# Moving operand sums between GpSimd and VectorE, and splitting layernorm steps over other ticks, in an attention + LoRA block

## The chip, the cores and the metric

One core of a Trainium2 chip runs the whole program. The metric is device microseconds of that core, the median of several runs. The engines are named as the profile names them: PE (TensorE), DVE (VectorE), ACT (ScalarE), POOL (GpSimd) and SP (SyncE, which issues the DMAs here).

## The reference

The input is 8 batches of 512 rows of 1024 numbers, all float32.

```
x = x + layernorm(attn(layernorm(x)) @ Wo)       # 16 heads of 64, rotary q and k, causal softmax
h = layernorm(x)
x = x + layernorm(h @ W.T + bias + use_lora * (h @ A[b].T) @ B[b].T)   # three adapters of rank 16
```

## The kernel before, in words

**Two phases.** The first runs 32 attention units (8 batches, 4 groups of 4 heads). A unit is 21 ticks long; at each tick a piece of the q, k, v products of the next unit is issued between the pieces of attention. The last unit has no next one, so PE runs attention alone there. The second phase (`with ExitStack() as a` on) multiplies by a 1024x1024 matrix 16 times: passes q = 0 to 7 are batch q times Wo, passes 8 to 15 are batch q-8 times the FFN weight. Each pass ends in layernorm and residual, row tile by row tile, during the pass after it; for q < 8 the rows are normed once more and transposed to be the operand of pass q+8.

**Products.** Each multiplication is done by a scheme of seven products in place of eight (Strassen, in Winograd's form), twice nested. The left operand is the weight (`LW`, tiles `wo_..`, `wf_..`), the right one the rows (`RX`, tiles R and T). Of its four quarters the weight has L11, L12, L21, L22 and the sums S1 = L21+L22, S2 = S1-L11, S3 = L11-L21 (in place of L21), S4 = L12-S2. The rows have R11, R12, R21, R22 and T1 = R12-R11, T2 = R22-T1, T3 = R22-R12 (in place of R12), T4 = R21-T2. Each of these tiles has seven slots: four sub-quarters and three sums of them, which `sub_left` (L665) and `sub_right` (L698) form inside a tile. `sum_left` (L677) forms one of four parts of an S tile, `sum_right` (L710) one of three pieces of a T tile (slots 0-1, 2-3, 4-6).

**Ticks and slots.** A pass has 49 ticks: seven groups of seven slots. The groups are, in ORDER, (L11,R11), (L12,R21), (L22,T4), (S1,T1), (S3,T3), (S2,T2), (S4,R22), so they begin at ticks 0, 7, 14, 21, 28, 35, 42. A slot is one sub-product of two matmuls of 256 columns. In SLOTS the sub-products use the accumulators b, a, c (this one still for the group before), c, d, b, a. Accumulator a has one buffer, as d has; b and c have two.

**Drains.** `Group.drain` empties them a tick after the sub-product: at slot 2 ACT copies a to `p1` (L847) and DVE forms `u2` = p1 + b (L843); at slot 3 DVE finishes the group before; at slot 6 DVE does three adds (p1 + b, + c, + d); at slot 0 of the next group ACT copies a (L854). So the next group's slot 1 waits for that copy, slot 5 (which goes on adding to b) for `u2`, slot 2 of the next group (which goes on adding to c) for the first of the adds to c, slot 4 of the next for that to d.

**What sets the order.** Every engine has its own queue in program order, written by `run(tick, filler)` (L528): at a tick come the PE events, then the sub-product and the drain of the one before, then the other events in the order in which they were entered. Nothing is scheduled by a tool. A tick number thus decides the order in a queue; the time comes from semaphores alone. An engine with an empty queue runs ahead of PE as far as its operands allow.

**What the change touches.** Before the last unit's run the first weight (Wo) and right operand (pass 0) are loaded on SP in the order L11, R11, L12, R21, R12, R22, L22, L21. POOL does all `sub_left` and the sums S1 and S3 there, and DVE does T1, T2, T4, T3 at the unit's ticks 18 to 21. S2 and S4 follow on POOL in pass 0. Four sums over the last heads' results (L499, POOL) and a store to memory end the unit. `plan_right` plans the right operand of the next pass: loads at ticks 10, 17, 24, 31, T1, T2, T4 at 38, 45, 52 and T3 at 63 (tick 14 of the pass itself). `plan_left` loads the second weight in pass 7 and plans its sums in passes 7 and 8. `load_ht` and `sub_ht` (L799, L800) bring the small LoRA operand `htb` with its differences on POOL; slot 4 of a pass's second group is the first to use it. `combine` (L860) adds whole 128x1024 result tiles, in pass q at ticks 18, 38 and 45 to 52; POOL does c21, DVE the rest. `plan_rows` plans the norms of a pass: for row tile t from tick k = 55 + 7t on (tick 6 + 7t of the next pass). `stats` forms bn statistics of two halves (L875), their aggregate (L878) on DVE, a square root on ACT (L880), reciprocal and scaled mean (L885, L887) on DVE; `norm` (L892, ACT) applies them to a half; `add_row` (L904, POOL) adds the residual; `store_rows` (L909, SP) stores it. For q < 8 a second norm follows (key `x`), then PE transposes (L918), ACT copies to `xT` (L922), the LoRA input product (L928) and the store of `xT` to `x1t` (L942). `plan_last` is the same for the last pass, by itself.

Of the kernel before, what the change touches and what calls it, by code (L numbers as in the profile page):

```python
# [13 lines left out]
ALU = mybir.AluOpType  # L14
# [4 lines left out]
B, S, E = 8, 512, 1024  # L19
# [6 lines left out]
HALF = 512  # L26
# [102 lines left out]
def sandwich_kernel(  # L129
# [589 lines left out]
    for u in range(U):  # L719
# [10 lines left out]
        else:  # L730
# [14 lines left out]
            for n in ("L11", "L12", "L22", "S3"):  # L745
                for k in range(4):
                    sub_left("wo", n, k, eng)
            for n in ("S1", "S3"):
                for h in range(4):
                    sum_left(wop, "wo", n, n, h, eng)  # L750
            for k, n in enumerate(("T1", "T2", "T4", "T3")):
                events[base + 18 + k].append(lambda n=n: sum_right(gp, 0, n, nc.vector))
# [8 lines left out]
    with ExitStack() as a:  # L761
# [109 lines left out]
        def stats(key, srcs, step):  # L871
# [4 lines left out]
            if step == 1:  # L876
                mv = small.tile([P, 2], F32, tag="mv", name=f"mv_{key}")
                nc.vector.bn_aggr(mv, ln[key])  # L878
                sd = small.tile([P, 1], F32, tag="sd", name=f"sd_{key}")
                nc.scalar.activation(sd, mv[:, 1:2], AF.Sqrt, bias=eps, scale=1.0)  # L880
                ln[key] = mv, sd
            if step == 2:
# [18 lines left out]
        def add_row(q, t, eng=None):  # L901
            for h, c in enumerate(halves(q, t)):
                e = eng or nc.gpsimd
                e.tensor_tensor(c, c, row[q, t][:, ts(h, HALF)], op=ALU.add)  # L904
# [57 lines left out]
        def plan_left(base):  # L962
# [13 lines left out]
            for n, tag, eng, ticks in (  # L976
                ("S1", "S3", pool, (43, 44, 45, 46)), ("S3", None, dve, (58, 61, 65, 68)),
                ("S2", "S2", pool, (57, 59, 61, 63)), ("S4", "S4", pool, (70, 72, 74, 76)),
# [9 lines left out]
        def plan_rows(q, base):  # L988

            for t in range(NT):  # L990
                k = base + 55 + 7 * t
                key = f"{'o' if q < B else 'y'}{q}_{t}"
                at(k, lambda t=t: load_row(q, t))
                for m in range(3):
                    at(k + m, lambda t=t, m=m, key=key: stats(key, halves(q, t), m))
                at(k + 3, lambda t=t, key=key: [norm(key, c, c) for c in halves(q, t)])
                at(k + 4, lambda t=t: add_row(q, t))
                at(k + 11, lambda t=t: store_rows(q, t))
                if q < B:
                    key = f"x{q}_{t}"  # L1000
                    for m in range(3):
                        at(k + 13 + m, lambda t=t, m=m, key=key: stats(key, halves(q, t), m))
                    at(k + 16, lambda t=t, key=key: [
                        norm(key, row[q, t][:, ts(h, HALF)], c) for h, c in enumerate(halves(q, t))
                    ])
# [189 lines left out]
```

## Time and profile before

| | |
|---|---|
| median of 3 runs | 2663.11 us (2663.02 to 2663.95) |
| the profiled execution's own time | 2664.64 us |
| its span, from the first to the last instruction | 2662.6 us |
| mean granted TensorE clock | 0.986 |
| second phase, first PE row | 1765.74 us |
| pass 7 and 8, POOL busy from 2154.90 to 2277.40 us | 120.83 of 122.50 us |
| PE busy in the same stretch | 92.39 us |

The page gives busy times of each engine, then the span in 40 slices of 66.6 us, each digit a busy share in tenths. A line of a timeline is: start, duration, engine, line, operation, output <- input, shape, count, and in brackets the idle time just before and the instruction that ended it. "+2 forms" or a count over one means that rows are merged, so a duration is that of all of them from the first's start. A line of the waits is: engine, tile and line that waited <- what it waited for: total us, times, longest.

### The profile page before, as it was taken

How to read it: one execution, taken by the hardware profiler on the slowest of the kernel's cores; microseconds unless marked ns; L12 is line 12 of the kernel's file. 1: busy time of each engine (PE TensorE's matmuls, PEld its weight loads, DVE VectorE, ACT ScalarE, POOL GpSimd, SP SyncE). 2: the span in 40 equal slices, each digit the busy share in tenths (PEclk: the TensorE clock that was granted, in tenths of full speed). 3: DMA queues.
4: the chain of work that ended last, by engine and by line, in shares of the span. 5: the costliest groups of instructions: out<-in, count | busy, mean ns of one | idle time of the engine just before them, and what ended most of it. 6: DMA issues, size and time to landing. Idle time of an engine off the chain costs nothing.

```text
span 2662.6 us, 40719 instructions
## 1 busy us (share of the span) xinstructions
PE 2544.0 (96%) x14656; PEld 2072.2 (78%) x14656; DVE 1577.5 (59%) x3702; ACT 1060.5 (40%) x2674; POOL 1534.2 (58%) x1141
## 2 busy tenths in 40 slices
PE   7999999999999999999999999969999986999997
PEld 6778777787778777878788778738777775888886
DVE  5655555554565455555565555446667665676666
ACT  1544444444454354444344434323434432322222
POOL 5364444436436436445443554386776699788885
PEclk9999999999999999999999999979999998999999
DMA  4232423423423333242342232235456562423433
GB/s 151 96 108 85 147 64 108 146 73 106 138 75 113 113 107 99 84 143 66 111 143 87 91 111 84 91 146 166 166 193 207 199 215 91 156 99 135 152 110 131
DMA packets 95130, 326.75 MB, mean 123 GB/s; under 512 B 16753, under 2 KB 18801, under 8 KB 77522
## 3 DMA queue, kind: packets, MB, share of 16 engines
q1 hardware_dynamic: 94930, 324.15, 36.7%
q8 instruction: 118, 1.93, 0.3%
q14 instruction: 82, 0.67, 0.1%
HBM read 208.74 MB, written 81.79 MB: 109 GB/s over the span
## 4 chain that ended last, share of the span: by engine, by line
PE 85%; DVE 7%; POOL 4%; issue 2%; ACT 1%; DMA 1%; SPq 0%; ACTq 0%; DVEq 0%; POOLq 0%
PE s L399 7%; PE ptp L455 6%; PE po L475 6%; PE accc_P L821 6%; PE acca_P L821 5%; PE accb_P L821 5%; PE acca_q L348 5%; PE acca_v L330 4%; PE accb_k L348 4%; PE accc_q L348 4%; PE accc_k L348 4%; PE acca_k L348 4%; PE accb_q L348 4%; PE accc_v L330 4%; PE accb_v L330 4%; PE accd_P L821 3%
## 5 line engine op out<-in xcount | busy, mean ns | idle before, releaser
L430 ACT ACTIVATE pr<-pr,nm 128x128 f32<-128x128 f32 (+3 forms) x512 | 282.2, 552 | 576.0 <-DVE nm L420 576.0
L441 ACT ACTIVATE pr<-pr,rs 128x128 f32<-128x128 f32 (+3 forms) x512 | 252.2, 552 | 161.1 <-DVE rs L438 161.1
L420 DVE CUSTOM_DVE_ANT_0 pr<-s,mask 128x128 f32<-128x128 f32 (+3 forms) x512 | 225.8, 488 | 92.1 <-PE s L399 91.4
L181 POOL TENSOR_TENSOR sv<-wv 128x512 f32<-128x512 f32 x32 | 40.6, 1269 | 316.1 <-PE accc_q L348 316.1
L904 POOL TENSOR_TENSOR c<-c,row 128x512 f32<-128x512 f32 x120 | 164.8, 1394 | 88.0 <-ACT c L892 85.0
L455 PE MATMUL ptp<-ident,pr 128*128 128x128 f32 x1280 | 186.2, 281 | 17.7 <-ACT pr L441 17.7
L399 PE MATMUL s<-k,q 64*128 64x128 f32 (+3 forms) x1024 | 193.0, 474 | 1.6 <-DVE nm L420 1.3
L710 POOL TENSOR_TENSOR T<-R,T 128x512 f32<-128x512 f32 (+1 forms) x90 | 165.5, 1866 | 38.8 <-PE accc_P L821 24.8
L455 PEld LDWEIGHTS ptp<-ident,pr 128*128 128x128 f32 x1280 | 147.6, 142 | 50.9 <-ACT pr L441 34.0
L181 POOL TENSOR_TENSOR sq<-wq 128x512 f32<-128x512 f32 x32 | 40.6, 1267 | 241.1 <-PE accc_k L348 234.9
L181 POOL TENSOR_TENSOR sk<-wk 128x512 f32<-128x512 f32 x32 | 41.3, 1290 | 198.5 <-PE accc_v L330 198.5
L475 PE MATMUL po<-pT,v 128*64 128x512 f32 (+3 forms) x1024 | 154.7, 443 | 0.0
L330 PEld LDWEIGHTS acca_v<-wv,R 128*128 128x128 f32 x1024 | 119.3, 192 | 23.6 <-issue 23.5
L467 DVE COPY pT<-ptp 128x384 f32<-128x384 f32 (+1 forms) x128 | 79.5, 621 | 95.0 <-PE ptp L455 92.4
L475 PEld LDWEIGHTS po<-pT,v 128*64 128x64 f32 x1024 | 69.0, 138 | 85.7 <-issue 71.6
L348 PE MATMUL acca_q<-R,wq 128*128 128x256 f32 x512 | 128.1, 393 | 0.0
L330 PE MATMUL acca_v<-wv,R 128*128 128x128 f32 x1024 | 127.9, 278 | 0.0
L348 PEld LDWEIGHTS acca_q<-R,wq 128*128 128x128 f32 x512 | 92.7, 191 | 44.0 <-issue 33.8
L843 DVE TENSOR_TENSOR p_P<-accb_P,p_P 128x256 f32<-128x256 f32 x112 | 46.9, 419 | 125.5 <-PE accb_P L821 71.2
L348 PE MATMUL acca_k<-R,wk 128*128 128x256 f32 x512 | 121.0, 379 | 0.0
L348 PEld LDWEIGHTS acca_k<-R,wk 128*128 128x128 f32 x512 | 96.7, 190 | 12.9
L399 PEld LDWEIGHTS s<-k,q 64*128 64x128 f32 x1024 | 73.2, 187 | 42.7 <-issue 34.7
(266 smaller groups left out, 6541.3 us busy)
## 6 DMA issues: line engine op xcount, KB each, us to landing
wq<-in_wq_dram SPq DMA_DIRECT2D x32, 1024.0 KB, 5.1
wk<-in_wk_dram SPq DMA_DIRECT2D x32, 1024.0 KB, 4.9
wv<-in_wv_dram SPq DMA_DIRECT2D x32, 1024.0 KB, 5.0
attn<-ops SPq DMA_DIRECT2D x16, 1792.0 KB, 7.9
R<-attn SPq DMA_DIRECT2D x32, 896.0 KB, 4.8
x<-in_x_dram SPq DMA_DIRECT2D x32, 512.0 KB, 7.4
row<-in_x_dram SPq DMA_DIRECT2D x32, 512.0 KB, 6.0
x<-c SPq DMA_DIRECT2D x64, 256.0 KB, 3.6
```

Source lines behind the costliest of these rows:

```text
L181: lambda eng: eng.tensor_tensor(s1, L21, L22, op=ALU.add),
L330: nc.tensor.matmul(acc[:, ts(c, P)], lhsT=R[right][:, k, ts(c, P)], rhs=L[left][:, k, :], start=(first and c == 0 and k == 0), stop=True, ...
L348: nc.tensor.matmul(acc, lhsT=L[left][:, k, :], rhs=R[right][:, k, :], start=(first and k == 0), stop=True, skip_group_check=True,)
L399: nc.tensor.matmul(ps[:, j, at : at + L], lhsT=qT[r, self.i, ts(qb, P)], rhs=kT[r, self.i, :L], start=True, stop=True,)
L420: nc.vector.tensor_tensor_reduce(out=v[:, j, :], in0=self.ps[qb][:, j, :], in1=mask[:, S - L :], scale=-1.0 / HD**0.5, scalar=3.0e38, op0= ...
L430: nc.scalar.activation(v[:, j, :], v[:, j, :], AF.Exp, bias=nm[:, j : j + 1], scale=-1.0, accum_out=sm[:, j : j + 1],)
L441: nc.scalar.mul(v, v, rs[:, j : j + 1])
L455: nc.tensor.transpose(pt[:, n, :], self.pr[qb][:, j, ts(kb, P)], ident)
L475: nc.tensor.matmul(po[j * HD : (j + 1) * HD, kb * P :], lhsT=v[:, kb, c : c + HD], rhs=self.pT[j][:, kb, kb * P :], start=(kb == 0), stop= ...
L710: eng.tensor_tensor(RX[q, n][:, c], RX[q, x][:, c], RX[q, y][:, c], op=ALU.subtract)
L821: nc.tensor.matmul(acc, lhsT=right[:, SLOT_R[r], k, :], rhs=left[:, SLOT_L[l], k, :], start=(first and k == 0), stop=True, skip_group_chec ...
L904: e.tensor_tensor(c, c, row[q, t][:, ts(h, HALF)], op=ALU.add)
```

## The change

The diff does four things.

- In the last attention POOL's queue gets T1, T2 and T4 of pass 0 between the differences of L12 and L22. S1 and S3 of the first weight leave it for DVE at ticks 15-18 and 20-23 of pass 0; S2 and S4 stay on POOL, at ticks 24 and 33 in place of 14 and 26; T3 goes to DVE at ticks 24 to 26 in three pieces.
- In `stats` the square root gets a step of its own, one tick after the aggregate. The steps of `plan_rows` move to suit: the halves' norms and adds stand at ticks of their own, the second norm's statistics begin at k+12 in place of k+13, rows are loaded at k+2 and stored at k+12.
- The second weight's S1 goes from POOL (ticks 43-46 of pass 7) to DVE (47, 50, 53, 54); the ticks of S3 and S2 move by one to two. Each sum is in four parts as before.
- For pass 8 alone, the LoRA operand is loaded at tick 10 of pass 7 and its differences formed at 16, in place of 52 and 53.

```diff
--- before.py
+++ after.py
@@ -742,14 +742,12 @@
             load_right(gp, 0, "R22")
             load_left(wop, wo, "wo", "L22", "L22")
             load_left(wop, wo, "wo", "L21", "S3")
-            for n in ("L11", "L12", "L22", "S3"):
-                for k in range(4):
-                    sub_left("wo", n, k, eng)
-            for n in ("S1", "S3"):
-                for h in range(4):
-                    sum_left(wop, "wo", n, n, h, eng)
-            for k, n in enumerate(("T1", "T2", "T4", "T3")):
-                events[base + 18 + k].append(lambda n=n: sum_right(gp, 0, n, nc.vector))
+            for n in ("L11", "L12", "T1", "T2", "T4", "L22", "S3"):
+                if n[0] == "T":
+                    sum_right(gp, 0, n, eng)
+                else:
+                    for k in range(4):
+                        sub_left("wo", n, k, eng)
             for k in range(PER + 1):
                 run(base + k, None)
             for k in sorted(events):
@@ -876,10 +874,13 @@
             if step == 1:
                 mv = small.tile([P, 2], F32, tag="mv", name=f"mv_{key}")
                 nc.vector.bn_aggr(mv, ln[key])
+                ln[key] = mv
+            if step == 2:
+                mv = ln[key]
                 sd = small.tile([P, 1], F32, tag="sd", name=f"sd_{key}")
                 nc.scalar.activation(sd, mv[:, 1:2], AF.Sqrt, bias=eps, scale=1.0)
                 ln[key] = mv, sd
-            if step == 2:
+            if step == 3:
                 mv, sd = ln[key]
                 rs = small.tile([P, 1], F32, tag="rstd", name=f"rstd_{key}")
                 nc.vector.reciprocal(rs, sd)
@@ -898,10 +899,9 @@
             src = x[q, ts(t, P), :] if q < B else x1d[q - B][:, t, :]
             nc.sync.dma_start(out=row[q, t], in_=src)
 
-        def add_row(q, t, eng=None):
-            for h, c in enumerate(halves(q, t)):
-                e = eng or nc.gpsimd
-                e.tensor_tensor(c, c, row[q, t][:, ts(h, HALF)], op=ALU.add)
+        def add_row(q, t, h):
+            c = halves(q, t)[h]
+            nc.gpsimd.tensor_tensor(c, c, row[q, t][:, ts(h, HALF)], op=ALU.add)
 
         def store_rows(q, t):
             for h, c in enumerate(halves(q, t)):
@@ -974,8 +974,8 @@
                         lambda n=n, m=m: sub_left("wf", "S3" if n == "L21" else n, m, pool),
                     )
             for n, tag, eng, ticks in (
-                ("S1", "S3", pool, (43, 44, 45, 46)), ("S3", None, dve, (58, 61, 65, 68)),
-                ("S2", "S2", pool, (57, 59, 61, 63)), ("S4", "S4", pool, (70, 72, 74, 76)),
+                ("S1", "S3", dve, (47, 50, 53, 54)), ("S3", None, dve, (59, 60, 66, 67)),
+                ("S2", "S2", pool, (58, 60, 62, 64)), ("S4", "S4", pool, (70, 72, 74, 76)),
             ):
                 for m in range(4):
                     at(
@@ -990,19 +990,21 @@
             for t in range(NT):
                 k = base + 55 + 7 * t
                 key = f"{'o' if q < B else 'y'}{q}_{t}"
-                at(k, lambda t=t: load_row(q, t))
-                for m in range(3):
+                at(k + 2, lambda t=t: load_row(q, t))
+                for m in range(4):
                     at(k + m, lambda t=t, m=m, key=key: stats(key, halves(q, t), m))
-                at(k + 3, lambda t=t, key=key: [norm(key, c, c) for c in halves(q, t)])
-                at(k + 4, lambda t=t: add_row(q, t))
-                at(k + 11, lambda t=t: store_rows(q, t))
+                for h in range(2):
+                    at(k + 4 + h, lambda t=t, h=h, key=key: norm(key, halves(q, t)[h], halves(q, t)[h]))
+                    at(k + 6 + h, lambda t=t, h=h: add_row(q, t, h))
+                at(k + 12, lambda t=t: store_rows(q, t))
                 if q < B:
                     key = f"x{q}_{t}"
-                    for m in range(3):
-                        at(k + 13 + m, lambda t=t, m=m, key=key: stats(key, halves(q, t), m))
-                    at(k + 16, lambda t=t, key=key: [
-                        norm(key, row[q, t][:, ts(h, HALF)], c) for h, c in enumerate(halves(q, t))
-                    ])
+                    for m in range(4):
+                        at(k + 12 + m, lambda t=t, m=m, key=key: stats(key, halves(q, t), m))
+                    for h in range(2):
+                        at(k + 16 + h, lambda t=t, h=h, key=key: norm(
+                            key, row[q, t][:, ts(h, HALF)], halves(q, t)[h]
+                        ))
                     for g in range(2):
                         at(k + 20 + g, lambda t=t, g=g: transpose_x1(q, t, g), "pe")
                         at(k + 20 + g, lambda pt, t=t, g=g: keep_x1(q, t, g, pt), "post")
@@ -1044,23 +1046,29 @@
                 at(base + 34, lambda t=t: load_row(q, t))
             for t in range(2):
                 at(base + 46 + t, lambda t=t: [ready(t, 0), ready(t, 1), moments_of(t)])
-                at(base + 47 + t, lambda t=t: [stats(f"y{q}_{t}", None, 2), end(t, 0, pool), end(t, 1, pool)])
+                at(base + 47 + t, lambda t=t: [stats(f"y{q}_{t}", None, 3), end(t, 0, pool), end(t, 1, pool)])
             at(base + 48, lambda: [load_row(q, 3), ready(2, 1)])
             at(base + 49, lambda: [sum_c12(0), ready(2, 0), moments_of(2), ready(3, 1)])
-            at(base + 52, lambda: [sum_c12(1), ready(3, 0), moments_of(3), stats(f"y{q}_2", None, 2),
-                                   stats(f"y{q}_3", None, 2)])
+            at(base + 52, lambda: [sum_c12(1), ready(3, 0), moments_of(3), stats(f"y{q}_2", None, 3),
+                                   stats(f"y{q}_3", None, 3)])
             at(base + 53, lambda: [end(2, 0, pool), end(2, 1, dve), end(3, 0, pool), end(3, 1, dve)])
 
-        for n, k in (("S2", 14), ("S4", 26)):
+        for n, k, eng in (
+            ("S1", 15, nc.vector), ("S3", 20, nc.vector), ("S2", 24, nc.gpsimd), ("S4", 33, nc.gpsimd)
+        ):
+            pool = wop if eng is nc.vector else wop2
             for h in range(4):
-                at(k + h, lambda n=n, h=h: sum_left(wop2, "wo", n, n, h, nc.gpsimd))
+                at(k + h, lambda n=n, h=h, eng=eng, pool=pool: sum_left(pool, "wo", n, n, h, eng))
+        for h in range(3):
+            at(24 + h, lambda h=h: sum_right(gp, 0, "T3", nc.vector, slice(h, h + 1)))
         for q in range(NQ):
             base = q * N2
             if q + 1 < NQ:
                 plan_right(q + 1, base)
             if q >= B - 1 and q + 1 < NQ:
-                at(base + 52, lambda q=q: load_ht(q + 1 - B))
-                at(base + 53, lambda q=q: sub_ht(q + 1 - B))
+                k = 10 if q == B - 1 else 52
+                at(base + k, lambda q=q: load_ht(q + 1 - B))
+                at(base + k + (6 if q == B - 1 else 1), lambda q=q: sub_ht(q + 1 - B))
             if q == B - 1:
                 plan_left(base)
             dve, pool = nc.vector, nc.gpsimd
```

## The prediction

> **What bounds the kernel now.** I read the page, then TensorE's waits from 1766 us on (the projection passes), then the timelines of all engines around each wait.
>
> ```profile
> PE 2544.0 (96%) x14656; PEld 2072.2 (78%) x14656; DVE 1577.5 (59%) x3702; ACT 1060.5 (40%) x2674; POOL 1534.2 (58%) x1141
> PE   7999999999999999999999999969999986999997
> ...
> POOL 5364444436436436445443554386776699788885
> ```
>
> TensorE (PE) is the bound; it falls off in slices 27 and 33-34, and in the latter POOL is full. Nothing can be won but PE's gaps. Those of the projection, as totals, counts and longest:
>
> ```profile
> PE acca_P L821 <- ACT c L854: 21.7, 16, 5.9
> PE accd_P L828 <- POOL htb L800: 21.5, 6, 15.3
> PE accb_P L821 <- DVE u_P L843: 13.9, 2, 13.7
> PE acca_P L821 <- ACT U L854: 11.3, 8, 6.0
> ```
>
> Gap A, at the start of pass 0 (start, duration, engine):
>
> ```profile
> 1754.13 8.19 POOL L677 TENSOR_TENSOR wo_S<-wo_L,wo_L 128x1024 f32<-128x1024 f32 x4
> 1766.46 5.72 DVE L710 TENSOR_TENSOR T<-R,R 128x512 f32<-128x512 f32 x3
> 1772.11 8.48 DVE L710 TENSOR_TENSOR T<-R,T 128x512 f32<-128x512 f32 x6
> 1780.51 2.15 DVE L710 TENSOR_TENSOR R<-R,R 128x512 f32<-128x512 f32 x3
> 1783.14 2.04 PE L821 MATMUL accb_P<-wo_L,R 128*128 128x256 f32 x4 [13.68 <-DVE u_P L843]
> 1785.09 8.19 POOL L677 TENSOR_TENSOR wo_S<-wo_S,wo_L 128x1024 f32<-128x1024 f32 x4 [5.17 <-DMA attn<-ops]
> ```
>
> Twelve right-operand sums stand on DVE ahead of the first drain, and PE idles 13.68 us. Gap B, once in each of passes 1 to 7 with two small ones:
>
> ```profile
> 1946.32 2.00 DVE L860 TENSOR_TENSOR c<-c,A 128x1024 f32<-128x1024 f32 x1
> 1950.68 0.21 DVE L878 BATCH_NORM_AGGREGATE mv_x<-bn_x 128x2 f32<-128x12 f32 x1
> 1950.92 0.29 ACT L880 ACTIVATE sd_x<-mv_x,eps 128x1 f32<-128x1 f32 x1 [3.74 <-DVE mv_x L878]
> 1951.12 0.35 ACT L854 COPY c<-acca_P 128x256 f32<-128x256 f32 x1
> 1951.53 1.13 PE L821 MATMUL acca_P<-wo_S,T 128*128 128x256 f32 x4 [1.59 <-ACT c L854]
> ```
>
> ACT holds a square root that waits for DVE; the copy that frees accumulator `a` stands behind it. Gaps C, passes 7 and 8:
>
> ```profile
> 2195.88 2.08 PE L821 MATMUL acca_P<-wo_S,R 128*128 128x256 f32 x4 [5.99 <-ACT U L854]
> 2224.67 6.21 POOL L710 TENSOR_TENSOR T<-R,T 128x512 f32<-128x512 f32 x3
> 2232.68 1.22 PE L828 MATMUL accd_P<-lb_sb,htb 128*128 128x256 f32 x2 [15.34 <-POOL htb L800]
> 2251.93 2.07 PE L821 MATMUL acca_P<-wf_S,T 128*128 128x256 f32 x4 [5.94 <-ACT c L854]
> ```
>
> From 2154.9 to 2277.4 POOL is busy 120.8 of 122.5 us: the stretch is POOL's.
>
> **What the Trainium skill says.** "SBUF — State Buffer", Who interferes with whom: a DVE instruction with two SBUF inputs and a GpSimd one that reads SBUF exclude each other, one blocking fully. The trace agrees: the 128x1024 combine takes 1.22 us at best and 2.0-2.2 beside POOL; T1's three pieces took 5.72 us beside POOL, T3's, alone, 2.15. Drains (one input in PSUM) stay at 0.41-0.43. "TensorE: Matmul & The Clock Gate", What's actually happening: an idle window of some 3.4 us halves PE's clock. Agrees: after the gaps of 6 us and more PE's first rows take 2.08 and 1.91 where 1.03 is usual, about 2.6 us lost each. Same page, Architectural detail: DVE and ACT are strict FIFOs; gap B shows it.
>
> A tick (two sub-products) is 0.863 us by PE's starts.
>
> **Startup (A).** Removed: the 9 pieces of T1, T2, T4 on DVE (5.72 + 8.48 us) and T3 there (2.15). POOL takes the nine in the last attention at 1.25, 1.25, 1.8 us a sum (a later T1 on POOL: 4.27), 12.9 in all, and is rid of S1 and S3 there (8.19 + 9.08, from 1754.13 to 1771.37). Its last weight differences would end near 1764 and the last heads' four sums, which wait for DVE's store at 1766.5, near 1772 instead of 1778.6: hidden by attention, unless the right operand's loads land after 1744, when L22, queued behind them on SP, had landed; each us later than about 2 us would then be one on the heads' sums, which pass 0 doesn't need. The first drain is at 1768.7; the 13.68 us and 2.6 of slow clock go. Added on DVE in ticks 15-26: S1, S3 (three parts of 1.15 and one of 0.6 each, 4.05), T3 (2.1), beside the combine of tick 18 (1.15). Behind them stand the drains, for which PE waits. POOL's S2 and S4 (2.3, 2.3, 2.3, 1.27 a sum) follow S1 part by part whatever their tick, since POOL is empty; they take turns with DVE. The walk, DVE's piece first wherever it is queued already: S1 starts 1777.6; S1 part 3 ends 1785.8; combine 1789.9 (behind a POOL part); S3 parts 1792.3, 1795.7, 1799.2, so the `u2` drain for tick 26 is at 1799.6, 6.4 us late; last piece of T3 between 1802 and 1805.5. Tick 28 needs that piece. Before it began at 1805.66, so 0 to 4 us are won, less 1-2 of slow clock after the new gap. I take **1 us**; the ends are +12 (POOL comes late and DVE runs alone: T3 ends at 1793) and -4 (each turn is a full POOL part and the clock falls twice).
>
> **Square roots (B).** Aggregate and square root keep a tick between them, and x statistics start a tick earlier, ahead of the combine. In the second and fourth tile the aggregate now precedes the three drains of its tick (1.2 us): gaps of 0.63 and 0.57 vanish. In the first, the statistic goes to tick 18, but the combine still waits for POOL's T3, itself 0.8 us later as the reciprocal moved: aggregate 0.7 us earlier, 1.59 becomes 0.9. Each half's norm costs 0.77 as before (1.52 a pair), between copies. Pass 1 gains 1.5 (its gap is 1.01), passes 2-6 1.9 each: **11 us**. Ends: 6 (the first tile gains nothing and one small gap stays) and 13 (all close). Adds, row loads and row stores move 1-4 ticks, hidden: tile t's add ends some 3 us before its statistics, as POOL idles 4-5 us per tile there.
>
> **The weight change (C).** Off POOL: S1 (5.65 + 3.56 = 9.2). The LoRA differences (0.72 + 0.99) move ahead, to tick 16; their load, on SP at tick 10, reads rows written in pass 1 and waits for nothing, so the row and weight loads behind it on SP lose only its issue (0.45 us, hidden by their slack). On DVE: S1, 4.05, each part excluding POOL. S1's second part needs L22's third difference from POOL, with `u2` of tick 51 queued behind it.
> - 5.99: the fourth tile's add now stands behind two weight differences more (2.5), the LoRA pair (1.7) and 0.8, so at 2193.7, not 2188.7; its statistics are asked for a tick earlier and hold DVE. PE's tick 43 stays at about 2196: gain 0. (The other cause, rows stored ahead of `x1t` on SP, goes, as they change places.)
> - 15.34: the LoRA operand is ready. Late next is T4 on POOL, before done at 2230.84: less 9.2, plus 2.5 (LoRA, reciprocal), plus 4.05 of blocking: 2228.2; walking the turns gives up to 2230.4. Tick 63 goes from 2237.19 to 2229.5: gain 7.7.
> - 5.94: add, S2 and S3 take turns as before; tick 71 from 2251.93 to between 2244 and 2248: gain 4-8 (T3's and S3's pieces stand in DVE's way as before; POOL reaches the first tile's add up to 8 us earlier).
> - 0.63 and 1.91 close, the third tile's add costs some 4: by tick 92 (2282.00 before) 8 to 12. I take **10 us**, pass 7's own B gaps included. Ends: 4 (S1's part waits and the drains with it) and 20 (no blocking: T4 at 2224, the rows' adds no more late).
>
> The words of the change speak of weight sums as single operations; the diff leaves each in four parts, so no gain from fewer instructions is counted.
>
> **The rest: 0.** From pass 9 on the LoRA operand stays at ticks 52/53 behind T2, combine and T4, so the five gaps of 1.23-1.25 stay; the tail's square roots were apart already. If one more thing went ahead of it on POOL, five times 1.25.
>
> **Sum.** 1 + 11 + 10 = 22 us. The profiled execution took 2664.64 (span 2662.6 and 2.0 around it), 1.5 above the median of three, 2663.11. 2664.64 - 22 = 2642.6; by the median, **2641**.
>
> **Rivals.**
> 1. Little blocking: DVE and POOL seldom meet. A 12, B 12, C 18: 42 us, 2621. For: every op fits its slot when alone. Against: T1's 0.95, 2.84 and 1.93 us in turns with POOL.
> 2. The square roots don't bind: combine, norm halves or the add stand where they stood. A 1, B 4, C 7: 12 us, 2651. For: the combine stays in front.
> 3. Slower: the shared port. DVE pays a full POOL part (2.3) before each moved sum, drains behind it. In A 11 pieces x 2.3 + 11.4 own + 3.8 drains from 1777.6 end T3 at 1818, 12 late; in C eight parts x 3.4 = 27 where S3's four stood, 13.6 more than before, 10 of it above what POOL gives back; B +11 only: 2674. It decides once T3's last piece ends after about 1816. Against: POOL has just eight parts there, 16.4 us.
>
> **Numbers.** Forecast 0.52 (its own range 2632-2648), rival 1 0.22, rival 2 0.19, rival 3 0.07. Lowest from the upper ends 12 + 13 + 20 = 45: 2618. Highest from 4 of C, 6 of B, -4 of A: 6, so 2657. Measurable is about 0.2%, 5.3 us, which the forecast and rival 1 clear and rival 2 mostly: faster 0.87, same 0.07, slower 0.06.
>
> **What would show it.** Right: no gap of 13 us, but two or three of 2-6 us between 1783 and 1803, with DVE's L677 above 2 us; gaps at the first tile below 1 us, at the others none; the 15.34 gone, T4's rows (L710) named or a shorter wait before tick 63. Wrong: DVE's S1 and S3 at 1.2 us each (rival 1), gaps of 1.59 still there (rival 2), PE behind 1806 at tick 28 (rival 3).

## The result and the profile after

The changed kernel takes 2636.65 us (median of four runs, 2635.30 to 2637.85) beside 2663.48 us for the kernel before on the same chip: a ratio of 0.9899, 95% interval 0.9882 to 0.9916. The forecast was 2641 us, with a range of 2632 to 2648. The profiled execution has a span of 2634.9 us (before: 2662.6), so 27.7 us are to be found in the trace. Below, "before" and "after" are the two kernels; line numbers of after are those of the changed file (the product is L819, its drains L841, L845 and L852, the combine L858, left sums L677, right sums L710, statistics L873, aggregate L876, square root L881, row adds L904, the LoRA differences L797 and L798).

The page's engine line and slices, after:

```profile
PE 2542.0 (96%) x14656; PEld 2071.4 (79%) x14656; DVE 1592.0 (60%) x3705; ACT 1063.6 (40%) x2674; POOL 1524.8 (58%) x1138
...
PE   7999999999999999999999999978999997999997
...
POOL 5364445446345345353553544467677689988875
```

PE's work is the same 14656 instructions. The dip in the last third is one slice of 7 where before had 8 and 6, and the dip at slice 27 is now a 7 and an 8: what PE won lies there and in the small waits between, which the slices don't show. POOL's slices of the last third are as full as they were (its busy time fell from 1534.2 to 1524.8 us): the change did not empty its queue. The sums S1 and S3 left it, and the nine pieces of T1, T2 and T4 came in. TensorE's waits from 1766 us on (what PE stood for, total, times, longest):

```profile
PE acca_P L819 <- ACT c L852: 11.7, 10, 6.0
PE accb_P L819 <- DVE u_P L841: 10.6, 3, 5.4
PE accd_P L826 <- POOL htb L798: 6.2, 5, 1.2
PE acca_P L819 <- ACT U L852: 4.2, 2, 3.9
```

The LoRA wait is down from 21.5 to 6.2 us (the one of 15.3 is gone, the five of 1.24 stay), the waits for ACT's copies of `c` from 21.7 to 11.7 and of `U` from 11.3 to 4.2.

**Where the 27.7 us came from**, by PE's first row of the same tick in both timelines:

| tick | before, us | after, us | won so far |
|---|---|---|---|
| tick 28 of pass 0 | 1805.66 | 1805.72 | -0.1 |
| tick 22 of pass 1 | 1844.39 | 1843.75 | 0.6 |
| tick 22 of pass 2 | 1897.96 | 1894.45 | 3.5 |
| tick 22 of pass 7 | 2165.88 | 2147.95 | 17.9 |
| tick 63 of pass 7 | 2237.19 | 2210.34 | 26.9 |
| tick 71 of pass 7 | 2251.93 | 2227.04 | 24.9 |
| tick 92 of pass 7 | 2282.00 | 2254.50 | 27.5 |

By these rows the start of the product gave -0.1, passes 1 to 6 gave 16.9 (17.9 less the 1.1 of pass 7's own first gap, counted from -0.1), passes 7 and 8 gave 10.7, and the rest 0.2.

The first of these terms holds a piece of chance. Pass 0 began at 1766.91 us in this execution and at 1765.74 in that of before; in the profiled executions of the later kernels with the same new start it began anywhere from 1764.51 to 1766.57. So the 1.2 us are scatter of the attention phase. Counted from pass 0's own first row, tick 28 comes after 38.8 us in after and after 39.9 in before: 1.1 us won there.

**The start.** DVE's timeline, then PE's rows that waited, in after (start, duration, engine, line, output <- inputs; x3 are three instructions in a row):

```profile
1778.71 1.22 DVE L677 TENSOR_TENSOR wo_S<-wo_L,wo_L 128x1024 f32<-128x1024 f32 x1
1783.75 3.85 DVE L677 TENSOR_TENSOR wo_S<-wo_L,wo_L 128x1024 f32<-128x1024 f32 x2
1787.53 3.36 DVE L858 TENSOR_TENSOR c<-c,A 128x1024 f32<-128x1024 f32 x1
1791.93 7.78 DVE L677 TENSOR_TENSOR wo_L<-wo_L,wo_L 128x1024 f32<-128x1024 f32 x3
1799.64 0.41 DVE L841 TENSOR_TENSOR u_P<-accb_P,p_P 128x256 f32<-128x256 f32 x1
1802.73 2.89 DVE L710 TENSOR_TENSOR R<-R,R 128x512 f32<-128x512 f32 x3
```

```profile
1787.06 2.07 PE L819 MATMUL accb_P<-wo_S,T 128*128 128x256 f32 x4 [2.61 <-DVE wo_S L677]
1791.83 1.10 PE L819 MATMUL accc_P<-wo_L,T 128*128 128x256 f32 x4 [1.20 <-DVE c L841]
1800.10 2.08 PE L819 MATMUL accb_P<-wo_S,T 128*128 128x256 f32 x4 [5.44 <-DVE u_P L841]
1805.72 1.10 PE L819 MATMUL accb_P<-wo_L,R 128*128 128x256 f32 x4 [1.83 <-issue]
```

POOL's S2 and S4 run at the same time:

```profile
1787.08 4.93 POOL L677 TENSOR_TENSOR wo_S<-wo_S,wo_L 128x1024 f32<-128x1024 f32 x2 [1.16 <-DVE wo_S L677]
1791.98 11.62 POOL L677 TENSOR_TENSOR wo_S<-wo_L,wo_S 128x1024 f32<-128x1024 f32 x4
```

The first part of S1 is alone and takes 1.22 us. Of S3's three large parts the first gets in just ahead of POOL and takes 1.22 us too; the other two wait for a part of POOL's each and take 3.37 and 3.35. This is the third:

```profile
1796.36 3.35 DVE L677 TENSOR_TENSOR wo_L<-wo_L,wo_L 128x1024 f32<-128x1024 f32 x1
```

The combine takes 3.36 us for the same reason. The drain `u_P` stands behind S3's parts on DVE, and PE behind the drain. One gap of 13.68 us has become four of 2.61, 1.20, 5.44 and 1.83.

**The norms.** Pass 3's first tile in after, DVE, ACT and PE:

```profile
1941.21 0.68 DVE L873 BATCH_NORM_STATS2 bn_x<-c 128x6 f32<-128x512 f32 x1
1941.81 1.84 DVE L858 TENSOR_TENSOR c<-c,A 128x1024 f32<-128x1024 f32 x1
1943.58 0.68 DVE L873 BATCH_NORM_STATS2 bn_x<-c 128x6 f32<-128x512 f32 x1
1944.29 0.21 DVE L876 BATCH_NORM_AGGREGATE mv_x<-bn_x 128x2 f32<-128x12 f32 x1
1944.42 0.37 DVE L841 TENSOR_TENSOR p_P<-accb_P,p_P 128x256 f32<-128x256 f32 x1
```

```profile
1944.54 0.29 ACT L881 ACTIVATE sd_x<-mv_x,eps 128x1 f32<-128x1 f32 x1 [2.02 <-DVE mv_x L876]
1944.74 0.35 ACT L852 COPY c<-acca_P 128x256 f32<-128x256 f32 x1
```

```profile
1945.14 1.13 PE L819 MATMUL acca_P<-wo_S,T 128*128 128x256 f32 x4 [0.46 <-ACT c L852]
```

The copy still stands behind a square root that waits for DVE, but the aggregate is now ahead of the drains of its tick, and PE waits 0.46 us instead of 1.59. The gaps of 0.63 and 0.57 of the second and fourth tile are gone from passes 2 to 6.

**Passes 7 and 8.** PE's rows that waited, in after:

```profile
2177.94 1.13 PE L819 MATMUL acca_P<-wo_S,R 128*128 128x256 f32 x4 [3.95 <-ACT U L852]
...
2196.57 2.05 PE L819 MATMUL accb_P<-wf_L,R 128*128 128x256 f32 x4 [3.79 <-DVE u_P L841]
2203.57 1.99 PE L819 MATMUL accc_P<-wf_L,R 128*128 128x256 f32 x8 [1.68 <-DVE A L841]
2210.34 1.13 PE L819 MATMUL accb_P<-wf_L,T 128*128 128x256 f32 x4 [0.89 <-POOL T L710]
2217.30 1.13 PE L819 MATMUL accb_P<-wf_L,T 128*128 128x256 f32 x4 [1.36 <-DVE u_P L841]
2227.04 2.07 PE L819 MATMUL acca_P<-wf_S,T 128*128 128x256 f32 x4 [6.02 <-ACT c L852]
```

The 15.34 us for the LoRA operand are replaced by a string of small waits, 3.79, 1.68, 0.89 and 1.36, and the 6 us at tick 71 are as they were. The 3.79 us are a wait for the drain `u2` of tick 51. It stands on DVE behind S1's second part, and that part waited for a difference from POOL:

```profile
2193.82 2.27 DVE L677 TENSOR_TENSOR wf_S<-wf_L,wf_L 128x1024 f32<-128x1024 f32 x1 [1.92 <-POOL wf_L L665]
```

### The profile page after: what moved, and what is told of

It is laid out like the page before. It is cut to its first block, busy times and chain, and to the rows that moved or that the text cites. A ratio compares the mean times of both kernels' runs of the same rounds, so it can differ in the third digit from the quotient of the medians.

```text
span 2634.9 us, 40686 instructions
## 1 busy us (share of the span) xinstructions
PE 2542.0 (96%) x14656; PEld 2071.4 (79%) x14656; DVE 1592.0 (60%) x3705; ACT 1063.6 (40%) x2674; POOL 1524.8 (58%) x1138
## 4 chain that ended last, share of the span: by engine, by line
PE 83%; POOL 7%; DVE 7%; issue 1%; ACT 1%; DMA 1%; SPq 0%; ACTq 0%; DVEq 0%; POOLq 0%
PE s L399 7%; PE ptp L455 6%; PE po L475 6%; PE acca_P L819 5%; PE acca_q L348 5%; PE accb_P L819 5%; PE accc_P L819 5%; PE acca_v L330 4%; PE accb_k L348 4%; PE accc_q L348 4%; PE accc_k L348 4%; PE acca_k L348 4%; PE accb_q L348 4%; PE accb_v L330 4%; PE accc_v L330 4%; PE accd_k L348 2%
## 5 line engine op out<-in xcount | busy, mean ns | idle before, releaser
L904 POOL TENSOR_TENSOR c<-c,row 128x512 f32<-128x512 f32 x120 | 161.7, 1368 | 84.0 <-ACT c L893 81.6
L455 PE MATMUL ptp<-ident,pr 128*128 128x128 f32 x1280 | 187.3, 282 | 17.9 <-ACT pr L441 17.9
L710 POOL TENSOR_TENSOR T<-R,T 128x512 f32<-128x512 f32 (+1 forms) x96 | 175.9, 1859 | 21.5 <-DVE u_P L841 20.3
L841 DVE TENSOR_TENSOR p_P<-accb_P,p_P 128x256 f32<-128x256 f32 x112 | 46.2, 412 | 100.4 <-PE accb_P L819 55.7
```

Of the source, the lines that this page charges most:

```text
L455: nc.tensor.transpose(pt[:, n, :], self.pr[qb][:, j, ts(kb, P)], ident)
L710: eng.tensor_tensor(RX[q, n][:, c], RX[q, x][:, c], RX[q, y][:, c], op=ALU.subtract)
L904: nc.gpsimd.tensor_tensor(c, c, row[q, t][:, ts(h, HALF)], op=ALU.add)
```

## The experiments

The theory under test is the prediction's: the start gains nothing, since DVE and POOL exclude each other there; the norms' steps give the largest share; the weight change gives its part because it relieves POOL. Each kernel was timed beside before; ratios are to before, with 95% intervals. After itself was timed with the result above and not again, so "faster" or "slower than after" is a difference of medians from different sessions. Before's own median moved by 0.7 us between them, and differences of 1 us or less are taken as nothing. The code fences show the main lines of each diff and leave out the rest.

### The three parts alone

Three kernels, each before with one part of the change. `e1_start_only` has the part in the last attention and ticks 15 to 36 of pass 0, `e2_rows_only` the aggregate, square root, norm halves, adds and row transfers, `e3_weight_only` the wf sums on DVE and the early LoRA operand:

```diff
e1:
-for n in ("L11", "L12", "L22", "S3"):
+for n in ("L11", "L12", "T1", "T2", "T4", "L22", "S3"):
-for n, k in (("S2", 14), ("S4", 26)):
+("S1", 15, nc.vector), ("S3", 20, nc.vector), ("S2", 24, nc.gpsimd), ("S4", 33, nc.gpsimd)
e2:
+if step == 2:
+    mv = ln[key]
-at(k + 13 + m, lambda t=t, m=m, key=key: stats(key, halves(q, t), m))
+at(k + 12 + m, lambda t=t, m=m, key=key: stats(key, halves(q, t), m))
e3:
-("S1", "S3", pool, (43, 44, 45, 46)), ("S3", None, dve, (58, 61, 65, 68)),
+("S1", "S3", dve, (47, 50, 53, 54)), ("S3", None, dve, (59, 60, 66, 67)),
-at(base + 52, lambda q=q: load_ht(q + 1 - B))
+k = 10 if q == B - 1 else 52
```

> Of the change only the startup part (T1, T2, T4 on POOL in the last attention; S1, S3 and T3 on DVE in pass 0). Theory (shared port: DVE's sums take turns with POOL's S2 and S4, and PE's drains stand behind them): the 13.7 us gap goes and as much comes back between ticks 21 and 28, so 0 us against before, within 3: about 2663. Rival (the startup part did gain, and something later in pass 0 to 8 ate it): 8 to 12 us faster, about 2653.

> Of the change only the moved steps of the norms (square root a tick after the aggregate, statistics of the second norm a tick earlier, halves apart). Theory (rows alone make 2.8 us a pass for passes 1 to 6 and something in 7): 16 to 19 us faster, about 2645. Rival (part of it was won only because POOL's and DVE's sums moved too): under 11 us, above 2652.

> Of the change only pass 7's part (second weight's S1 on DVE, LoRA differences at tick 16). Theory: the 15.3 us gap gives way to shorter waits for POOL's T4 and for DVE's u2; 8 to 12 us faster, about 2653. Rival (what passes 7 and 8 won came from the rows' steps): under 4 us.

Measured: the start 2665.13 us, 1.0004 (0.9996 to 1.0013), no difference; the norms' steps 2642.07 us, 0.9918 (0.9902 to 0.9935), 21.8 us faster, where 16 to 19 were expected; the weights and LoRA 2655.30 us, 0.9972 (0.9963 to 0.9981), 8.6 us faster. Together they would be 29.2, the whole change is 26.8 (medians). The 2.4 between them are no overlap that the runs show: the last part's interval alone runs from 5 to 10 us, and in the profiled executions the three spans differ from before's by +0.2, -20.9 and -6.4, together -27.1, beside -27.7 for the whole.

In the first kernel the start's 1.1 us are won and lost again. Tick 28 comes 38.8 us after pass 0's first row there too. But PE's granted clock was still halved (0.50 from 1804.0 to 1807.7), and its next two rows took 2.04 and 1.91 us, where after's took 1.10 and 1.03. At tick 22 of pass 1 this kernel is 0.9 us behind before, both counted from pass 0's first row.

The norms' steps are the largest share. By tick 22 of pass 7 they won 18.2 us, and 20.3 by tick 92. In that kernel (the lines here are numbered as in before) passes 7 and 8 show what they are without the relief of POOL:

```profile
2215.78 1.22 PE L828 MATMUL accd_P<-lb_sb,htb 128*128 128x256 f32 x2 [18.53 <-POOL htb L800]
```

18.53 us, where before had 15.34: PE came earlier and waited for the same POOL.

### Is the start's zero the shared port? S2 and S4 held back

`e4_pool_held` is after with S2 and S4 of the first left operand queued behind a tiny POOL operation that reads T3's last piece and writes a column that nothing uses:

```diff
-("S2", 24, nc.gpsimd), ("S4", 33, nc.gpsimd)
+("S2", 28, nc.gpsimd), ("S4", 33, nc.gpsimd)
+at(27, lambda: nc.gpsimd.tensor_tensor(
+    scr, RX[0, "T3"][:, 6, 1, 0:1], RX[0, "T3"][:, 6, 0, 0:1], op=ALU.add))
```

> The changed kernel, with POOL's S2 and S4 of the first weight held back until DVE has done the last piece of T3 (a sum of one column of T3 into a scratch tile, which is left unused, put ahead of S2 on POOL). Theory (shared port): DVE's S1 and S3 parts then take 1.2 us in place of 2.3 to 2.6, T3's last piece ends near 1794 in place of 1805.6, tick 28 starts 8 to 11 us earlier; S2 then ends near 1803 where tick 35 wants it near 1801, S4 near 1811 where tick 42 wants it near 1807: net 4 to 8 us faster than the changed kernel, about 2630. Rival (DVE simply has too much in front of its drains, whoever runs beside it): parts stay above 2 us or the gaps stay, no gain, 2636 or more.

Measured: 2635.77 us, 0.9895 (0.988 to 0.991), 0.9 us better than after. The local half of the theory holds: S3's three parts take 3.49 us, 1.16 each, and PE's row of tick 28 starts at 1792.95, 12.8 us earlier than in after. But the 4 to 8 us that were expected of it did not come. By tick 22 of pass 1 only 0.5 is left (1843.30 beside 1843.75); the rest is lost in PE's waits:

```profile
1800.10 1.13 PE L819 MATMUL accb_P<-wo_S,T 128*128 128x256 f32 x4 [0.86 <-POOL wo_S L677]
1808.24 1.13 PE L819 MATMUL accb_P<-wo_S,R 128*128 128x256 f32 x4 [1.84 <-POOL wo_S L677]
1821.90 2.07 PE L819 MATMUL acca_P<-wo_L,R 128*128 128x256 f32 x4 [6.48 <-ACT A L852]
```

The longest is DVE's, whose timeline in the same kernel shows one combine of 9.77 us, and POOL's beside it:

```profile
1811.60 9.77 DVE L858 TENSOR_TENSOR U<-U,A 128x1024 f32<-128x1024 f32 x1
```

```profile
1809.38 4.25 POOL L710 TENSOR_TENSOR T<-R,R 128x512 f32<-128x512 f32 x3
1813.60 2.48 POOL L858 TENSOR_TENSOR c<-c,c 128x512 f32<-128x512 f32 x2
1816.04 4.23 POOL L710 TENSOR_TENSOR T<-R,T 128x512 f32<-128x512 f32 x3
1821.53 4.47 POOL L858 TENSOR_TENSOR c<-c,U 128x512 f32<-128x512 f32 x2 [1.25 <-DVE U L858]
```

While DVE's combine stood, POOL ran the end of one operation and six more back to back at their unhindered length. The combine, 1.22 us when alone, ended only when POOL ran out of work that didn't need its result. My reading is that holding all of POOL's sums had made a backlog, and that the backlog kept the port that the two engines share.

### Only S4 held

`e10_s4_held` leaves S2 at its place and holds S4 alone. Its room is the 11 us in which POOL stands idle in after between S4 and the next right operand's T1:

```diff
+at(28, lambda: nc.gpsimd.tensor_tensor(
+    scr, RX[0, "T3"][:, 6, 1, 0:1], RX[0, "T3"][:, 6, 0, 0:1], op=ALU.add))
```

> After, with only S4 of the first left operand held on GpSimd until the first right operand's T3 is done on VectorE (a one-column operation that reads T3's last piece and writes an unused column, 0.2 us); S2 keeps its place. Theory: S4's four parts cost VectorE's S3 and T3 a turn each; without them S3's parts take 1.2 us, T3 ends near 1799 and tick 28 starts 5 to 6 us earlier, near 1800; S4 then runs from 1799 to 1807.5, in the 11 us in which GpSimd stood idle, and PE needs it after 1812; GpSimd's next sums wait for PE as in after, so no long run of its operations meets VectorE's combine. 5 to 6.5 us faster than after: 2630 to 2632. Rival: what is won is given back as it was when both S2 and S4 were held (a combine on VectorE kept waiting 6 us and more by GpSimd's backlog): within 1.5 us of after, 2635 to 2638.

Measured: 2628.86 us, 0.9867 (0.9853 to 0.9882), 7.8 us faster than after. DVE and PE in that kernel:

```profile
1790.72 3.49 DVE L677 TENSOR_TENSOR wo_L<-wo_L,wo_L 128x1024 f32<-128x1024 f32 x3
...
1795.39 2.15 DVE L710 TENSOR_TENSOR R<-R,R 128x512 f32<-128x512 f32 x3
```

```profile
1797.64 1.10 PE L819 MATMUL accb_P<-wo_L,R 128*128 128x256 f32 x4 [0.78 <-issue]
```

S3's three parts take 3.49 us instead of 7.78, T3 2.15 instead of 2.89, and tick 28 comes 8.1 us earlier than in after, of which 1.2 were there when the rows of S1 began (1785.84 beside 1787.06). So 6.9 us are the held S4's. POOL's T1 there starts at 1806.65, and from then on no combine of DVE takes more than 2.2 us. By tick 22 of pass 1 the lead is 8.0 (1835.75 beside 1843.75): nothing is given back, and a little more came than the 5 to 6.5 us expected. So what kept the start from gaining was S4 colliding with S3 and T3, and it was avoidable. S2 still collides with S1 there: the combine at 1786.31 takes 3.37 us as in after.

### The pieces of the weight change taken back

`e5_lora_late` is after with pass 8's LoRA operand back at ticks 52 and 53, `e6_s1_pool` after with the S1 of wf back on POOL at ticks 43 to 46:

```diff
e5:
-k = 10 if q == B - 1 else 52
-at(base + k, lambda q=q: load_ht(q + 1 - B))
+at(base + 52, lambda q=q: load_ht(q + 1 - B))
-at(base + k + (6 if q == B - 1 else 1), lambda q=q: sub_ht(q + 1 - B))
+at(base + 53, lambda q=q: sub_ht(q + 1 - B))
e6:
-("S1", "S3", dve, (47, 50, 53, 54))
+("S1", "S3", pool, (43, 44, 45, 46))
```

> The changed kernel, with the LoRA operand for pass 8 back at ticks 52 and 53. Theory (T4 on POOL was next in line, so the early load saves only what htb stood behind it): PE waits at tick 60 until htb, behind T4 at 2210, is done near 2212, and finds T4 ready: 2 to 6 us slower than the changed kernel, about 2641. Rival (the LoRA load is the whole gain of passes 7 and 8): 10 us slower or more, 2647.

> The changed kernel, with the second weight's S1 back on POOL at ticks 43 to 46. Theory (POOL's queue sets passes 7 and 8; S1 costs POOL 8 to 9 us and DVE's ports 4): T4 and the rows' adds come 4 to 5 us later on POOL, but PE no longer waits 3.8 and 1.7 us for drains behind S1 on DVE: 2 to 6 us slower, about 2640. Rival (S1 on DVE costs as much as it saves): within 1 us of the changed kernel. Second rival: faster, as the waits for u2 and A go and nothing else comes.

Measured: LoRA late 2637.22 us, 0.9901 (0.9886 to 0.9916), 0.6 slower than after, which the runs can't tell from nothing; S1 on POOL 2641.86 us, 0.9918 (0.9903 to 0.9933), 5.2 slower, as expected. With LoRA late, PE's waits are these:

```profile
2211.65 1.22 PE L826 MATMUL accd_P<-lb_sb,htb 128*128 128x256 f32 x2 [6.63 <-POOL htb L798]
2228.82 1.13 PE L819 MATMUL acca_P<-wf_S,T 128*128 128x256 f32 x4 [2.34 <-ACT c L852]
```

6.63 us for the operand, and 2.34 instead of 6.02 at tick 71: once S1 is off POOL, the early operand only changes the name of the wait, since the right operand's sums beside it on POOL are needed next. Counted from tick 22 of pass 7 this kernel is 7.0 us later than after at tick 63, 1.5 at tick 71 and 0.1 at tick 92. My expectation of 2 to 6 missed that. With S1 on POOL the early operand is worth no more: the kernel with S1 back and the operand early (2641.86) is as fast as the norms' steps alone, with both as in before (2642.07); the former also has the new start, which is worth nothing by itself, and S2 and S3 a tick or two away.

### The norms' steps taken apart

`e7_stats_13` is after with the second norm's statistics back where they began before (k + 13), the square root still a tick behind its aggregate; `e8_sqrt_joined` is after with the square root in the aggregate's step, the early statistics kept:

```diff
e7:
-at(k + 12 + m, lambda t=t, m=m, key=key: stats(key, halves(q, t), m))
+at(k + 13 + m, lambda t=t, m=m, key=key: stats(key, halves(q, t), m))
-at(k + 16 + h, lambda t=t, h=h, key=key: norm(
+at(k + 17 + h, lambda t=t, h=h, key=key: norm(
e8:
-    ln[key] = mv
-if step == 2:
-    mv = ln[key]
```

> The changed kernel, with the second norm's statistics at k+13 as before the change (square root still one tick after the aggregate, its norm at k+17, k+18). The root then stands behind the copy that frees accumulator a, not ahead of it. Theory (order in ACT's queue): the last gap of 0.46 us at the first tile goes too, seven times; 2 to 4 us faster than the changed kernel, about 2633.5. Rival (the earlier statistics closed the gaps, ahead of the combine and the three adds): gaps of 0.6 and 1.6 come back, 12 to 16 us slower.

> The changed kernel, with the square root back in the aggregate's own step (so a tick earlier in ACT's queue), all else as changed. Theory: the root waits for the same aggregate in front of the same copy, which needs both a tick later, so nothing changes for the second norm: within 1.5 us of the changed kernel, about 2636.6. Rival (the root's own tick is what closes the gaps): most of the 16 us comes back, 2650.

Measured: 2637.68 us, 0.9902 (0.9887 to 0.9917), 1.0 slower than after, where 2 to 4 faster was expected; and 2639.40 us, 0.9910 (0.9893 to 0.9926), 2.7 slower, where no change was. With the later statistics the root stands behind the copy. The gaps behind ACT's copies don't come back, and the first tile's last 0.46 goes as expected. But a new gap appears once a pass, the transposes waiting for the norm that is now a tick later, and a pass takes 51.05 us instead of 50.70:

```profile
1950.60 0.66 PE L918 MATMUL ptf<-ident,row 128*128 128x128 f32 x4 [0.91 <-ACT row L893]
```

With the square root joined again, the first tile's gap is the same 0.46, and a pass takes 51.11 us. The 0.41 more lie at ticks 25 to 29. There ACT's queue has the next tile's square root a tick earlier, ahead of the norm that the transposes need, and it waits for its aggregate:

```profile
1948.41 0.29 ACT L878 ACTIVATE sd_o<-mv_o,eps 128x1 f32<-128x1 f32 x1 [2.34 <-DVE mv_o L876]
```

In six passes this is 2.5 of the 2.7 us. So either half of the edit closes nearly all of the gaps behind the copies: the root a tick behind its aggregate, or the statistics a tick ahead. They aren't additive, and neither is the cause alone. Both kernels keep the halves' norms, the adds and the row transfers at their new ticks; no run puts these back, so what they give by themselves is not shown.

### The five small LoRA gaps, and both mends together

The prediction noted that five gaps of 1.24 us would go if the LoRA pair went ahead of one more thing on POOL. `e9_lora_51` does that for the operands of passes 9 to 15, and `e11_both` adds the held S4. (The expectation below speaks of passes 9 to 13 and of a place ahead of T2 and the combine. The gaps lie in passes 10 to 14, and the edit puts the pair behind T2 and the combine, ahead of T4 alone.)

```diff
-k = 10 if q == B - 1 else 52
-at(base + k, lambda q=q: load_ht(q + 1 - B))
-at(base + k + (6 if q == B - 1 else 1), lambda q=q: sub_ht(q + 1 - B))
+at(base + (10 if q == B - 1 else 51), lambda q=q: load_ht(q + 1 - B))
+at(base + (16 if q == B - 1 else 51), lambda q=q: sub_ht(q + 1 - B))
```

> After, with the load and the two differences of the LoRA operand of passes 9 to 13 moved from ticks 52 and 53 to tick 51, so that on GpSimd they stand ahead of T2's pieces, the combine and T4's. Theory: the five gaps of 1.23 to 1.25 us before the LoRA products are the pair's place in GpSimd's queue and nothing else; T4, which the pair (some 1.75 us) then delays, is needed only ten ticks later. All five go: 6.2 us faster than after, 2630.5. Rival: as with the pass-8 operand put back, the wait only changes its name, because the right operand's sums behind the pair are next in line; then the time stays within 1.5 us of after's, 2635 to 2638.

> Both of the edits to after at once: the LoRA pair at tick 51 and S4 held until T3 is done. They act at different places (passes 8 to 13, and pass 0), so by theory their gains add: some 12 us faster than after, 2624 to 2626. Rival: pass 7's GpSimd-bound stretch absorbs what pass 0 wins, since the rows of pass 1 and the weights arrive at times of their own; then only the LoRA gaps' 6 us are left, 2630.5.

Measured: 2628.58 us, 0.9867 (0.985 to 0.9883), 8.1 us faster than after, where 6.2 were expected; and 2621.00 us, 0.9839 (0.9824 to 0.9853), 15.7 us faster than after and the fastest version here. The gains add up: 7.8 and 8.1 against 15.7. POOL's order around the pair, with the pair at tick 51:

```profile
2319.00 0.72 POOL L797 TENSOR_TENSOR htb<-htb 128x256 f32<-128x256 f32 x1
2319.80 1.00 POOL L798 TENSOR_TENSOR htb<-htb 128x384 f32<-128x384 f32 x1
2320.75 4.27 POOL L710 TENSOR_TENSOR T<-R,T 128x512 f32<-128x512 f32 x3
```

T4 is behind the pair instead of ahead of it, and nobody waits for T4. The five gaps are worth more than their length: 5 x 1.24 = 6.2 of idle time, but 7.6 in the trace (8.1 by the spans, of which 0.5 were there at tick 22 of pass 7, 2147.43 beside 2147.95). After the wait the first LoRA row takes 0.70 us where the others take 0.59, and from the LoRA row before it to this one PE needs 9.61 us in after (2315.95 to 2325.56) and 8.21 without the wait (2315.47 to 2323.68): 1.40 for a wait of 1.24. The row after it then follows 0.54 us later, and 0.43 without the wait, another 0.11. That is 1.51 a gap, 0.27 more than the wait, and 7.6 for the five.

## Why the prediction was right, by its steps

The direction, the mechanisms and the sum were right, 27 us against 22; one of the three terms, the norms' steps, was too small by half of itself.

**A, the start: 1 forecast, -0.1 measured at tick 28, or 1.1 counted from pass 0's own first row.** The walk of turns was right in its mechanism. The Trainium skill says that the two engines exclude each other ("SBUF — State Buffer", Who interferes with whom), and the trace agrees. In the walk the second and third part of S3 each wait for one of POOL's and end 3.4 and 3.5 us after the part before; in after it was 3.3 and 3.3. That it also hits the time of day is in part luck. The `u2` drain forecast for 1799.6 ran at 1799.64, and T3's last piece, forecast between 1802 and 1805.5, ended at 1805.6; but S1 began at 1778.71, 1.1 us after the 1777.6 of the walk, because pass 0 began late, and the turns, a little shorter than walked, took 0.6 back by S3's third part. The 1 to 2 us of slow clock that the sum set aside fell behind tick 28 in the kernel with the start alone, and not there in after. The upper end given was +12, PE's row at 1793 with POOL out of the way; the held kernel put it at 1792.95. That hardly any of it would reach the total with all of POOL's sums held was not foreseen; with S4 alone held, some 7 us did.

**B, the square roots: 11 forecast, 16.9 measured.** This term was mis-sized, beyond its upper end of 13. Per pass it was 0.69 + 0.63 + 0.57 = 1.9; a pass got shorter by 2.87 (53.57 to 50.70). Two pieces were missing. (1) In the first tile the aggregate was taken to be 0.7 us earlier. The combine does wait for POOL's T3 as said, but the aggregate also moved ahead of the three drains of its tick, 1.2 us, as I had seen for the second and fourth tile and not for the first: the gap fell to 0.46 and not to 0.9, another 0.44. (2) A gap was priced at its idle time. PE's rows in before show what else it costs:

```profile
1948.04 1.03 PE L821 MATMUL acca_P<-wo_L,T 128*128 128x256 f32 x4
1948.91 1.03 PE L821 MATMUL accb_P<-wo_S,T 128*128 128x256 f32 x4
1951.53 1.13 PE L821 MATMUL acca_P<-wo_S,T 128*128 128x256 f32 x4 [1.59 <-ACT c L854]
1952.49 1.03 PE L821 MATMUL accc_P<-wo_L,T 128*128 128x256 f32 x4
```

In a stream a row of 1.03 us hands over after 0.86, so 0.17 of it overlaps the next row; at a gap this overlap is lost. And the row after the gap hands over after 0.96, 0.10 later. So a gap costs 0.27 us on top of its idle time, and by the same count the gaps of 0.63 and 0.57 cost that too. These two closed altogether in each pass, which is the other 0.54; it is also PE's busy time, 50.77 us a pass before and 50.23 after. Six passes at 0.44 + 0.54 are 5.9, which with 11 makes 16.9. The experiments add that the part does not hang on one edit: the later root alone or the earlier statistics alone keep most.

**C, the weight change: 10 forecast, 10.7 measured.** Of its steps, counted from the 17.9 us that PE was already ahead at tick 22 of pass 7: tick 43 gained nothing as forecast (2195.88 to 2177.94, 17.9); tick 63 gained 8.9 where 7.7 were forecast, with T4 late next as named, a wait of 0.89; tick 71 gained 7.0 in all where 4 to 8 were forecast; tick 92 gained 9.6 where 8 to 12 were, and pass 7's own first gap makes it 10.7. Part of this comes from the norms' steps, which alone gain 2.1 between ticks 22 and 92 and the same first gap. What carries the weight change is S1 off POOL, 5.2 us when put back, and not the LoRA operand's early load, 0.6, though the profile of before named that operand for the 15.34 us. The 3.79 us behind S1's second part are the wait that the prediction had named. I had counted nothing for it on its own; it lies inside the 8.9.

**The rivals.** Little blocking (2621) falls: two of S3's three large parts took 3.4 us. Square roots that don't bind (2651) fall: 21.8 us alone. The shared port making it slower (2674) falls: POOL had only eight parts there, and T3 ended at 1805.6, far from the 1816 from which that was to decide. That an engine does pay a full part of the other's was right in this rival, and in the forecast too.

Still open: why DVE's combine was kept out for 9.77 us in the one kernel while it got a turn after each POOL operation in the others. The traces show the two patterns and not what chooses between them, and no run here isolates it.

## What to carry to other kernels

When two engines exclude each other, moving work from one to the other pays only if the other's own work is moved out of the window too: here S1, S3 and T3 on DVE brought nothing until S4 went into POOL's next idle stretch, and then some 7 us; but hold back only what fits into that idle stretch, since a larger backlog comes back as a wait. The longest wait that the profile of before named was only the last in a queue: ask what is next in the same queue before counting such a wait as won (15.34 us were named for the LoRA operand, 0.6 were its own). And a gap of about a microsecond on a busy TensorE is worth more than its length (2.33 us of idle time closed a pass gave 2.87), so that many small ones, repeated each pass, add up: here to the largest share of the gain.

## What the runs showed of the hardware

- A DVE operation with two SBUF inputs is usually let in after one POOL operation. A part of 1.2 us took 3.25 to 3.37 in after where it queued behind a POOL part of 2.3, and POOL's own parts took 3.3 to 3.4 instead of 2.35 in the same turns. In one kernel a combine was kept out for 9.77 us, by the end of one POOL operation and six more in a row. Turns can't be counted on.
- A gap in PE's stream of rows costs 0.27 us more than its idle time, counted by the rows' starts: 0.16 or 0.17 of lost overlap and 0.10 or 0.11 in the row after it. This came out the same for gaps of 0.57 to 1.59 us.
- The clock: in after the granted clock is halved from 1786.87 to 1790.28, 1797.11 to 1803.94, 2179.40 to 2182.81, 2196.47 to 2199.88 and 2223.77 to 2230.60 us. These stretches last 3.41 us or twice that, and their starts lie 10.24, 382.29, 17.07 and 27.30 us apart, which is 3, 112, 5 and 8 times 3.41. So the clock changed on a grid of 3.41 us only, and where a short gap lay on it seems to have decided whether a slow row followed. In after the idle 2.61 us ahead of S1's first row, from 1784.45 to 1787.06, lay almost whole in one step of the grid (1783.46 to 1786.87), and the row took 2.07 us. With S4 alone held, where the halved stretch at 1791.47 gives the grid, the same gap was cut at 1784.64 and the row took 1.13. After 5.44 and 6.02 us of idle the first row took 2.08 and 2.07, as after the long gaps of before. The Trainium skill has this window free-running ("TensorE: Matmul & The Clock Gate", What's actually happening), so that it doesn't start with the kernel; the two traces agree. How much of a step must be idle is not measured here.
